# Turning a gated activation by VectorE and small transfers instead of TensorE's transposes

## The chip, the cores and the metric

The kernel runs on one core of one Trainium2 chip. The time is device time in microseconds (us) of one execution, the median of several. Five engines work side by side, each through its own queue of instructions in order: TensorE (PE; its weight loads are shown as PEld), VectorE (DVE), ScalarE (ACT), GpSimd (POOL) and SyncE (SP). SP issues most transfers (DMAs), GpSimd those that accumulate into what they write.

## The reference

Two layers are added to x (8 sequences of 256 tokens, 1024 features). The first is a dense weight plus a mixture of eight low-rank experts, two of them chosen for each token; the second is a dense weight chosen for each sequence.

```python
def _L0_cond_ref(x, language_ids, W, Wr, A, B):       # A: 8 experts x 16 ranks x 1024
    base = jnp.einsum('btd,od->bto', x, W)
    logits = jnp.einsum('btd,ed->bte', x, Wr)
    logits = logits + bias[:, None, :]
    topw, topi = jax.lax.top_k(logits, 2)
    weights = jax.nn.softmax(topw, axis=-1)
    gates = jnp.sum(jax.nn.one_hot(topi, E) * weights[..., None], axis=-2)
    h = jnp.einsum('btd,erd->bter', x, A)
    lora_out = jnp.einsum('bter,bte,eor->bto', h, gates, B)
    return base + SCALING * lora_out

x = x + _L0_cond_ref(x, itok_B_0_7, W, Wr, A, B)
x = x + jnp.einsum('bsi,boi->bso', x, weight[itok_B_0_15])
```

Everything is in 32-bit floats.

## The kernel before

The first layer is one product of 2048 tokens with a 1024 x 1024 weight, done in seven block products after Strassen and Winograd. The tokens fall into two halves of 1024 (j = 0, 1), the features into two halves, so x is four blocks `x11`, `x12`, `x21`, `x22`, and W (with the identity added, which brings in "x +") is four blocks of weights. `opening` does product 1, `product(key, ...)` the others, in the order 2, 5, 6, 3, 7, 4. The sums of x blocks that Winograd's form needs (T1 to T4) are made in place by GpSimd's accumulating transfers: T1 is `x12 += x11` (two copies, line 1018), T2 is `x22 += x12`; `raw` (line 1028) and `add_raw` (line 1022) reload and add x from DRAM for T3 and T4. Output blocks of tokens of half 1 are kept with the sign turned, so what the low-rank part adds there must be turned too.

Inside each product there is a second level of the same scheme: `make_subs` lists VectorE's differences (`s1` to `s4` of weights, `t1` to `t4` of x), and some of its products ("leaves" 2, 3, 4) get a third level, whose differences are `r1` to `r4` and `q1` to `q4` and whose seven matmul pairs are `piece(1)` to `piece(7)`. Matmuls of 128x512 are at line 556, pieces at line 470, VectorE's sums and differences at line 228 (`tt`). `put` and `take` add finished banks of PSUM to the output blocks y (named A6, B5, X2, A7, B3, A4 after the bank and the second-level product).

The low-rank part. `project(j, c)` (line 256) computes for 512 tokens at a time A x and the router's logits together, tokens on the partitions. `take(j, c)` adds the bias to the logits and lets ScalarE copy A x into `hT[j]`: 128 tokens on the partitions, 8 chunks of tokens, 128 columns (8 experts x 16 ranks). `gating(j)` is a list of some 20 small VectorE steps that find the two best experts and their gates, and ends with `onto_h`, one multiply of 128x1024 that puts the gates on `hT[j]`. To use it as the right side of a matmul it must be turned, so that experts and ranks lie on the partitions and tokens in the columns: `turn(j, banks)` does so with 8 TensorE transposes into two banks (line 326) and two ScalarE copies into `hg[j]`, with a factor -1 for half 1. From there on `mm` adds the low-rank part into the same banks as the dense product:

```python
if up is not None and rows is not None:
    steps += [(up[rows][:, ts(m, P)], hg[tokens][:, c, :], m) for m in ms]
```

Half 0 is used in product 2 first, half 1 in product 5 first. `turn(0, ...)` is called after the last projection and before product 2; half 1's gating waits in a queue, and product 2 calls `turn_1` between its leaves.

The order of VectorE's work is planned when the program is built. `now` holds a planner's clock for TensorE and VectorE; `queue` holds work with the events it needs; `ahead` takes from the queue whatever is due before TensorE gets further; `force` takes a piece of work, and all before it that is free, at once. `product` puts its own late differences (`own`) at the head of the queue. [...]

Storage is reused closely: `hT[0]` and `hT[1]` lie in the first half of block `y22`, which product 5 writes; the gating's small tables lie in `y12`.

Of the kernel before, what the change touches and what calls it, by code (L numbers as in the profile page):

```python
# [9 lines left out]
F32 = mybir.dt.float32  # L10
I32 = mybir.dt.int32
AF = mybir.ActivationFunctionType
ALU = mybir.AluOpType
# [3 lines left out]
P = 128  # L17
# [8 lines left out]
def kernel(  # L26
# [62 lines left out]
    def flat(blk):  # L89
        return blk.rearrange("p k n -> p (k n)")  # L90

    def pair(name, n):

        return psum.tile([P, 2, TQ], F32, name=name, tag=f"pair{n}")
# [5 lines left out]
    def halves(pair_):  # L100
        return [pair_[:, v, :] for v in range(2)]
# [21 lines left out]

    aw_sb = flat(yb["12"])[:, : KC * EA].rearrange("p (k e) -> p k e", k=KC)
    hT = [flat(yb["22"])[:, j * C * ER : (j + 1) * C * ER].rearrange("p (c e) -> p c e", c=C) for j in range(2)]

    small = {}

# [92 lines left out]
    def copy(out_, x, scale=1.0):  # L221
        if scale == 1.0:
            nc.scalar.copy(out_, x)
        else:
            nc.scalar.activation(out_, x, AF.Copy, scale=scale)  # L225
# [13 lines left out]
        add(d, d, ident.unsqueeze(1).to_broadcast([P, k1 - k0, P]))  # L239


    hg = [const.tile([ER, 2, TQ], F32, name=f"hg{j}") for j in range(2)]
    lg = [rtile([P, C, E], f"lg{j}") for j in range(2)]
    gate8 = {}

# [43 lines left out]

    def gating(j):  # L290

        m1, hot1, ops1 = first_max(lg[j], j, 1)
        rest = rtile([P, C, E], "rest")
        m2, hot2, ops2 = first_max(rest, j, 2)
        dm = rtile([P, C], "dm")
        ex = rtile([P, C], "ex")
        den = rtile([P, C], "den")
        g1 = rtile([P, C], "g1")
        g2 = rtile([P, C], "g2")
        wide = [P, C, E]  # L300

        def onto_h():
            h = hT[j].rearrange("p c (e r) -> p (c e) r", r=R)
            g = hot1.rearrange("p c e -> p (c e)").unsqueeze(2).to_broadcast([P, C * E, R])
            tt(h, h, g, ALU.mult)


        ops = ops1 + [
            lambda: nc.vector.scalar_tensor_tensor(rest, hot1, NEG, lg[j], ALU.mult, ALU.add)
        ] + ops2 + [  # L310
            lambda: minus(dm, m2, m1),
            lambda: nc.scalar.activation(ex, dm, AF.Exp),
            lambda: nc.vector.tensor_scalar(den, ex, 1.0, None, ALU.add),
            lambda: nc.vector.reciprocal(g1, den),
            lambda: nc.vector.tensor_scalar(g1, g1, SCALING, None, ALU.mult),
            lambda: tt(g2, g1, ex, ALU.mult),
            lambda: tt(hot1, hot1, g1.unsqueeze(2).to_broadcast(wide), ALU.mult),
            lambda: tt(hot2, hot2, g2.unsqueeze(2).to_broadcast(wide), ALU.mult),
            lambda: add(hot1, hot1, hot2),
        ]  # L320
        return [(0.26, f) for f in ops] + [(us(2 * TQ), onto_h)]

    def turn(j, banks):

        for n in range(C):
            nc.tensor.transpose(banks[n // CQ][:, ts(n % CQ, P)], hT[j][:, n, :], ident)  # L326
        for c, ps_g in enumerate(banks):
            copy(hg[j][:, c, :], ps_g, -1.0 if j else 1.0)


    bdiff = const.tile([ER, OG + 3 * OQ], F32, name="bdiff")
# [19 lines left out]
    def us(n):  # L351
        return (n + 66) / 960

    def vec(t, fn, key=None):
        fn()
        now["dve"] += t
        done[key] = now["dve"] + 0.1

    def event(name, later=0.0):
        events[name] = now["pe"] + later  # L360
# [56 lines left out]
    def third(key, leaf, lhs, rhs, place, what):  # L417

        ra = lambda i, j: lhs()[:, j, ts(i, P)]
        rb = lambda i, j: rhs()[:, i, ts(j, NQ)]
        n0, n1 = slice(0, NQ), slice(NQ, TQ)
        t, own = {}, {}
        at = {"r13": 0, "r2": P, "r4": 2 * P, "q13": 3 * P, "q2": 3 * P + NQ, "q4": 3 * P + 2 * NQ}
        me = f"{key}:L{leaf}"

        def op(name, tag, fn, x, y, what):
            width = P if name[0] == "r" else NQ

            def run():
                if place == 0:
                    t[name] = sub3.tile([P, width], F32, name=f"{name}_{key}{leaf}", tag=tag)
                elif place == 3:
                    t[name] = flat(yb["12"])[:, 2048 + at[tag] : 2048 + at[tag] + width]
                else:
                    t[name] = spare(1536 + (place - 1) * 1152 + at[tag], width)
                fn(t[name], *(t[v] if isinstance(v, str) else v() for v in (x, y)))

            return us(width), what, f"{me}.{name}", run  # L440

        A, B = (lambda i, j: lambda: ra(i, j)), (lambda i, j: lambda: rb(i, j))
        ops = [
            op("r1", "r13", add, A(1, 0), A(1, 1), what),
            op("q1", "q13", minus, B(0, 1), B(0, 0), what),
            op("r2", "r2", minus, "r1", A(0, 0), what),
            op("q2", "q2", minus, B(1, 1), "q1", what),
            op("r4", "r4", minus, A(0, 1), "r2", what),
            op("q4", "q4", minus, B(1, 0), "q2", what),
        ]  # L450
        ops3 = [
            op("r3", "r13", minus, A(0, 0), A(1, 0), (f"{me}.5",)),
            op("q3", "q13", minus, B(1, 1), B(0, 1), (f"{me}.5",)),
        ]

        def piece(n, acc=None, banks=None, fresh=False):
            if n in (1, 5):
                own[n] = (single(f"P{n}_{key}{leaf}", n // 5) if banks is None else banks[n // 5])[:, n0]
            for x in {3: ("r4",), 4: ("q4",), 5: ("r1", "q1"), 6: ("r2", "q2", "P1"), 7: ("r3", "q3", "P6")}.get(n, ()):
                force(f"{me}.{x}")  # L460
            out_, l, r = {
                1: lambda: (own[1], ra(0, 0), rb(0, 0)),
                2: lambda: (acc[:, 0, n0], ra(0, 1), rb(1, 0)),
                3: lambda: (acc[:, 0, n1], t["r4"], rb(1, 1)),
                4: lambda: (acc[:, 1, n0], ra(1, 1), t["q4"]),
                5: lambda: (own[5], t["r1"], t["q1"]),
                6: lambda: (own[1], t["r2"], t["q2"]),
                7: lambda: (own[1], t["r3"], t["q3"]),
            }[n]()
            nc.tensor.matmul(out_, lhsT=l, rhs=r, start=(n in (1, 5) or fresh and n in (2, 4)), stop=True, skip_group_check=True)  # L470
            now["pe"] += 0.432
            event(f"{me}.{n}", 0.2)

        def take(n, dest, base=None, sub=False):

            cut = lambda v: {1: v[:, 0, n0], 6: v[:, 0, n1], 5: v[:, :, n1]}[n]
            if n == 7:
                cut = lambda v: v[:, 1, :].rearrange("p (j n) -> p j n", j=2)
            src = own[5 if n == 5 else 1]
            if n in (5, 7):  # L480
                src = src.unsqueeze(1).to_broadcast([P, 2, NQ])
            evict(NQ if n in (1, 6) else TQ, cut(dest), src, None if base is None else cut(base), f"{me}.P{n}", sub)

        return ops, ops3, piece, take
# [61 lines left out]
    def multiply(up=None, tokens=None):  # L546


        def mm(acc, lhs, rhs, first=False, rows=None, c=0, part=(0, 1), ms=(0, 1), need=()):
# [1 line left out]
                force(key)  # L551
            steps = [(lhs[:, k, ts(m, P)], rhs[:, k, :], m) for k in part for m in ms] if part else []
            if up is not None and rows is not None:
                steps += [(up[rows][:, ts(m, P)], hg[tokens][:, c, :], m) for m in ms]
            for i, (l, r, m) in enumerate(steps):
                nc.tensor.matmul(  # L556
                    acc[:, m, :],
# [132 lines left out]
        out(5, q2, q2)  # L690
        add(q2, A, q2)

    def product(key, base, dest, lora=None, tokens=None, sub=False, joined=None, between=None):

# [16 lines left out]
        own = list(deep[2][1]) if 2 in deep else []  # L713
        own += late[:1] + (deep[3][0] if 3 in deep else []) + late[1:] + (deep[4][0] if 4 in deep else [])
        own += (deep[3][1] if 3 in deep else []) + (deep[4][1] if 4 in deep else [])
        queue[:0] = own
        A = new("A")
        mm(A, a(0, 0), b(0, 0), True)
        X = new("X")
        nc.scalar.copy(X, A)  # L720
        if 2 in deep:
            _, _, piece, take = deep[2]
            piece(1)
            take(1, at[0], old[0], sub)
            B = new("B")
            mm(B, t["s1"], t["t1"], True, "1", 1, ms=(0,), need=K("s1", "t1"))
            piece(5)
            mm(A, t["s2"], t["t2"], need=K("s2", "t2"))
            event(f"{key}:P6", 0.2)
# [26 lines left out]
        if 4 in deep:  # L756
            _, _, piece4, take4 = deep[4]
            piece4(1)
            take4(1, at[2], old[2], sub)
        if between is not None:  # L760
            between(X)
        if 3 in deep:
            hold[0] = key
            _, _, piece, take = deep[3]
# [278 lines left out]
    project(1, 1, singles("ps_h_1_1"))  # L1043
    now["pe"] += 7.5
    force("gates0")
    turn(0, halves(pair("ps_g_0", 2)))
    after(0.4, lambda: take(1, 1))
    now["pe"] += 1.8
    for k in (0, 2):
        add_x("12", "11", k, k + 2)  # L1050
    event("T1", 17.0)
# [1 line left out]
        add_x("22", "12", k, k + 2)  # L1053
    event("T2", 30.0)
    queue += [(t, (), f"gate{i}", f) for i, (t, f) in enumerate(gating(1))]
    gates = queue[-1][2]
    queue += make_subs("5", "21", "12", (2, 3, 4), ("T1",), "2", 1)

    def turn_1(X):
        force(gates)  # L1060
        turn(1, halves(X))
        now["pe"] += 1.8

    product("2", y21, y11, 0, 0, between=turn_1)
    raw("21", 0, 1)
    add_raw("21", 1, 1)
    event("T3", 30.0)
# [21 lines left out]
        y0[:] = y0 or prep_y(0)  # L1089
        y0[i][2]()  # L1090

    queue += [(0.6, ("4:P7", "7:join2"), f"4.y{i}", lambda i=i: prep_y0(i)) for i in range(4)]
    product("4", y21, y21, 1, 0)
    for q in list(queue):
        q[3]()
# [58 lines left out]
```

## Time and profile before

| | |
|---|---|
| Median of 3 runs | 424.83 us (424.72 to 425.22) |
| The profiled execution | 424.31 us, of which the span from first to last instruction 422.2 |
| TensorE's granted clock | 1.000 |
| Data moved by transfers | 72.61 MB, mean 172 GB/s |

A span is cut into 40 slices of 10.55 us; each digit is the busy share of a slice in tenths:

```profile
PE   8999999999999999999999999999999999999996
DVE  1977879968789999978799565765657666665531
DMA  8995099576220946928903483765558384640202
```

The transfers' row falls to 0 in the fifth slice (42 to 53 us): the loads of the first layer are done and T1 has not begun. VectorE is at 9 in the slices from 84 us on, in which products 2 and 5 meet. A timeline line reads: start, duration of the group, engine, line, operation, output and inputs by name, size, number of instructions, and in brackets how long the engine was idle before and what ended that. Matmul starts are 0.43 us apart for 128x512, although each is shown 0.59 us long.

### The profile page before, as it was taken

To read this page: it belongs to the slowest core of one execution; us is meant where nothing else is said; L and a number is where in the kernel's file an instruction comes from. 1 tells how busy PE (TensorE), PEld (TensorE's weight loads), DVE (VectorE), ACT (ScalarE), POOL (GpSimd) and SP (SyncE) were. 2 spreads that over 40 slices of the span, in tenths; PEclk is the share of its full clock that TensorE was granted. 3 is DMA by queue.
4 is the path that set the end of the run, shared out by engine and by line. 5 is a ranking of instruction groups with operands and counts; after the bars stand their busy time and mean duration, and the time that the engine had idled before them with its cause. 6 is when DMAs were issued, how large, how long until landed. Compare 5 with 4: busy or idle time off the path is not lost.

```text
span 422.2 us, 3674 instructions
## 1 busy us (share of the span) xinstructions
PE 417.1 (99%) x1318; PEld 230.7 (55%) x1318; DVE 304.8 (72%) x489; ACT 40.9 (10%) x73; POOL 17.6 (4%) x26
## 2 busy tenths in 40 slices
PE   8999999999999999999999999999999999999996
PEld 6679975555655554554555444444444444444574
DVE  1977879968789999978799565765657666665531
ACT  2020130112110000000000101010101101010110
POOL 1000020110001101103000000000000000000000
PEclk9999999999999999999999999999999999999999
DMA  8995099576220946928903483765558384640202
GB/s 273 384 397 245 0 186 199 127 186 101 99 99 8 166 140 165 262 57 165 332 0 102 150 313 134 263 224 211 199 201 296 113 307 178 229 170 2 99 0 99
DMA packets 20257, 72.61 MB, mean 172 GB/s; under 512 B 1552, under 2 KB 3856, under 8 KB 15248
## 3 DMA queue, kind: packets, MB, share of 16 engines
q1 hardware_dynamic: 15088, 58.87, 38.4%
q0 software_dynamic: 3904, 12.58, 16.5%
q10 hardware_dynamic: 1248, 0.93, 0.7%
q8 instruction: 10, 0.16, 0.2%
q14 instruction: 7, 0.06, 0.1%
HBM read 55.61 MB, written 8.39 MB: 152 GB/s over the span
## 4 chain that ended last, share of the span: by engine, by line
PE 99%; POOL 0%; ACT 0%; issue 0%; POOLq 0%
PE A L908 23%; PE A L556 20%; PE B L908 13%; PE B L556 11%; PE ps_h L256 7%; PE X L908 7%; PE P L470 6%; PE A_last L975 3%; PE X L470 3%; PE X L556 3%; PE A L470 2%; PE B L470 1%; PE idle L573 1%; PE X L326 0%; PE ps_g L326 0%; ACT z L1005 0%
## 5 line engine op out<-in xcount | busy, mean ns | idle before, releaser
L556 PE MATMUL A<-t,s 128*128 128x512 f32 x112 | 50.3, 592 | 0.0
L908 PE MATMUL B<-x,x 128*128 128x512 f32 x96 | 43.2, 592 | 0.0
L228 DVE TENSOR_TENSOR w<-w,w 128x1024 f32<-128x1024 f32 x24 | 29.0, 1223 | 15.1 <-PE A L908 15.1
L908 PE MATMUL A<-w,x 128*128 128x512 f32 x88 | 39.6, 592 | 0.0
L908 PE MATMUL A<-w,y 128*128 128x512 f32 x88 | 39.1, 592 | 0.0
L256 PEld LDWEIGHTS ps_h<-y,x 128*128 128x128 f32 x256 | 31.7, 190 | 2.9 <-issue 2.4
L556 PEld LDWEIGHTS A<-t,s 128*128 128x128 f32 x112 | 21.2, 190 | 20.8 <-issue 20.1
L256 PE MATMUL ps_h<-y,x 128*128 128x136 f32 x256 | 31.9, 279 | 0.0
L908 PEld LDWEIGHTS B<-x,x 128*128 128x128 f32 x96 | 18.2, 190 | 22.1 <-issue 21.8
L228 DVE TENSOR_TENSOR y<-A,y 128x1024 f32<-128x1024 f32 x18 | 22.0, 1222 | 9.3 <-PE A L556 5.8
L908 PEld LDWEIGHTS A<-w,x 128*128 128x128 f32 x88 | 16.7, 190 | 21.0 <-issue 21.0
L908 PEld LDWEIGHTS A<-w,y 128*128 128x128 f32 x88 | 16.7, 190 | 20.6 <-issue 20.6
L228 DVE TENSOR_TENSOR y<-P,y 128x512 f32<-128x512 f32 (+1 forms) x37 | 21.1, 572 | 8.0 <-PE P L470 6.2
L556 PE MATMUL A<-x,w 128*128 128x512 f32 x56 | 25.3, 592 | 0.0
L228 DVE TENSOR_TENSOR x<-w,x 128x1024 f32<-128x1024 f32 (+1 forms) x12 | 10.9, 911 | 10.8 <-PE A L908 7.8
L228 DVE TENSOR_TENSOR w<-x,w 128x1024 f32<-128x1024 f32 x8 | 9.7, 1225 | 10.2 <-PE A L908 5.6
L225 ACT ACTIVATE z<-A 128x512 f32<-128x512 f32 x12 | 7.2, 597 | 101.0 <-PE A L908 101.0
L228 DVE TENSOR_TENSOR z<-z,X 128x512 f32<-128x512 f32 x7 | 4.8, 687 | 15.9 <-PE X L908 15.9
L556 PEld LDWEIGHTS A<-x,w 128*128 128x128 f32 x56 | 10.4, 190 | 10.3 <-issue 10.0
L556 PE MATMUL B<-x,s 128*128 128x512 f32 x32 | 14.9, 592 | 0.0
L228 DVE TENSOR_TENSOR x<-x 128x1024 f32<-128x1024 f32 (+1 forms) x15 | 14.7, 1005 | 0.0
L720 ACT COPY X<-A 128x1024 f32<-128x1024 f32 x6 | 6.0, 997 | 89.8 <-PE A L556 89.8
(203 smaller groups left out, 591.6 us busy)
## 6 DMA issues: line engine op xcount, KB each, us to landing
x<-w_dram SPq DMA_DIRECT2D x24, 1024.0 KB, 5.5
x<-xT_dram SPq DMA_DIRECT2D x10, 1024.0 KB, 11.0
w<-w_dram SPq DMA_DIRECT2D x8, 1024.0 KB, 4.7
out_dram<-z SPq DMA_DIRECT2D x15, 512.0 KB, 3.0
x<-x POOLq DMA_DIRECT2D x4, 1024.0 KB, 9.9
x<-xT_dram POOLq DMA_DIRECT2D x4, 1024.0 KB, 9.1
y<-y POOLq DMA_DIRECT2D x8, 512.0 KB, 5.1
w<-wT_dram SPq DMA_DIRECT2D x3, 1024.0 KB, 15.1
```

What stands on the lines that cost most here:

```text
L225: nc.scalar.activation(out_, x, AF.Copy, scale=scale)
L228: nc.vector.tensor_tensor(out_, x, y, op)
L256: nc.tensor.matmul(ps[v][:, u * EA : (u + 1) * EA], lhsT=xk(k, j, c)[:, ts(r, P)], rhs=aw_sb[:, k, :], start=(first and k == some[0] and u ...
L470: nc.tensor.matmul(out_, lhsT=l, rhs=r, start=(n in (1, 5) or fresh and n in (2, 4)), stop=True, skip_group_check=True)
L556: nc.tensor.matmul(acc[:, m, :], lhsT=l, rhs=r, start=(first and i < len(ms)), stop=(i >= len(steps) - len(ms)), skip_group_check=True,)
L573: nc.tensor.matmul(idle[:, 0, :P], lhsT=ident, rhs=ident, start=True, stop=True)
L720: nc.scalar.copy(X, A)
L908: nc.tensor.matmul(accs[name], lhsT=lhs[:, k // 2, k % 2, :], rhs=rhs[:, k, :], start=(first and k == 0), stop=(k == KH - 1), skip_group_c ...
L975: nc.tensor.matmul(acc, lhsT=lhs[:, k // 2, k % 2, :], rhs=rhs[:, k, ts(v, m)], start=(first and k == 0), stop=(k == KH - 1), skip_group_c ...
```

## The change

The turn of `hT[j]` no longer uses TensorE. VectorE turns each square of 32 x 32 by itself (one instruction for all of a half) into `squares[j]`, in the second half of block `y22`; 16 transfers of 32 partitions x 256 values, issued by SP, move the squares to the partitions where they belong. The layout of `hg[j]` becomes 4 groups of partitions-to-be x 8 chunks x 32 tokens, and `turned(j, c)` reads 512 tokens of it in runs of 32. The factor -1 of half 1 goes into the gates.

Further parts of the same change:

- `turn(j)` is now the last entry of `gating(j)`, so it is done by VectorE's order: for half 0 ahead of the differences of product 2, for half 1 out of the queue.
- Ahead of T1's transfers GpSimd copies one column of `hg[0]`, and so waits for all 16 landings of half 0.
- `product` puts its own late work behind those entries of the queue that begin with its key, and ahead of the others. In product 2 the first half of B's matmuls, with its low-rank part, stands ahead of `piece(1)`; in the others behind it as before.
- VectorE's work gives events too (`vec`), and `r3` and `q3` of a leaf wait for `r2` and `q2` as well.
- The sums of y for the first adapter wait for the last piece of leaf 3 in product 4 instead of its seventh second-level product.

```diff
+    QS = P // 4
+    squares = [flat(yb["22"])[:, (2 + j) * C * ER : (3 + j) * C * ER] for j in range(2)]
...
-    hg = [const.tile([ER, 2, TQ], F32, name=f"hg{j}") for j in range(2)]
+    hg = [const.tile([ER, 4, C, QS], F32, name=f"hg{j}") for j in range(2)]
...
-            lambda: nc.vector.tensor_scalar(g1, g1, SCALING, None, ALU.mult),
+            lambda: nc.vector.tensor_scalar(g1, g1, -SCALING if j else SCALING, None, ALU.mult),
...
-        return [(0.26, f) for f in ops] + [(us(2 * TQ), onto_h)]
-
-    def turn(j, banks):
-
-        for n in range(C):
-            nc.tensor.transpose(banks[n // CQ][:, ts(n % CQ, P)], hT[j][:, n, :], ident)
-        for c, ps_g in enumerate(banks):
-            copy(hg[j][:, c, :], ps_g, -1.0 if j else 1.0)
+        return [(0.26, f) for f in ops] + [(us(2 * TQ), onto_h), (us(2 * TQ), lambda: turn(j))]
+
+    def turn(j):
+
+
+        nc.vector.transpose(squares[j], hT[j].rearrange("p n (b r) -> p b n r", b=4))
+        v = squares[j].rearrange("p (b n) -> p b n", b=4)
+        for a in range(4):
+            for b in range(4):
+                nc.sync.dma_start(
+                    hg[j][b * QS : (b + 1) * QS, a].rearrange("p n q -> p (n q)"), v[a * QS : (a + 1) * QS, b]
+                )
+
+    def turned(j, c):
+        return hg[j][:, :, c * CQ : (c + 1) * CQ, :].rearrange("p a n q -> p n a q")
...
-        done[key] = now["dve"] + 0.1
+        done[key] = events[key] = now["dve"] + 0.1
...
-            op("r3", "r13", minus, A(0, 0), A(1, 0), (f"{me}.5",)),
-            op("q3", "q13", minus, B(1, 1), B(0, 1), (f"{me}.5",)),
+            op("r3", "r13", minus, A(0, 0), A(1, 0), (f"{me}.5", f"{me}.r2")),
+            op("q3", "q13", minus, B(1, 1), B(0, 1), (f"{me}.5", f"{me}.q2")),
...
-                steps += [(up[rows][:, ts(m, P)], hg[tokens][:, c, :], m) for m in ms]
+                steps += [(up[rows][:, ts(m, P)], turned(tokens, c), m) for m in ms]
...
-        queue[:0] = own
+        rest = list(queue)
+        queue[:] = [q for q in rest if q[2].startswith(key)] + own + [q for q in rest if not q[2].startswith(key)]
...
             _, _, piece, take = deep[2]
+            B = new("B")
+            if key == "2":
+                mm(B, t["s1"], t["t1"], True, "1", 1, ms=(0,), need=K("s1", "t1"))
             piece(1)
             take(1, at[0], old[0], sub)
-            B = new("B")
-            mm(B, t["s1"], t["t1"], True, "1", 1, ms=(0,), need=K("s1", "t1"))
+            if key != "2":
+                mm(B, t["s1"], t["t1"], True, "1", 1, ms=(0,), need=K("s1", "t1"))
...
-        if between is not None:
-            between(X)
...
     force("gates0")
-    turn(0, halves(pair("ps_g_0", 2)))
     after(0.4, lambda: take(1, 1))
-    now["pe"] += 1.8
+
+    landed = const.tile([ER, 4], F32, name="landed")
+    nc.gpsimd.tensor_copy(landed, hg[0][:, :, 0, 0])
     for k in (0, 2):
         add_x("12", "11", k, k + 2)
...
-    product("2", y21, y11, 0, 0, between=turn_1)
+    product("2", y21, y11, 0, 0)
...
-    queue += [(0.6, ("4:P7", "7:join2"), f"4.y{i}", lambda i=i: prep_y0(i)) for i in range(4)]
+    queue += [(0.6, ("4:L3.7", "7:join2"), f"4.y{i}", lambda i=i: prep_y0(i)) for i in range(4)]
```

More of the change, by code (lines that the diff above doesn't have):

```diff
@@ L691, in opening, with product @@
         add(q2, A, q2)
-    def product(key, base, dest, lora=None, tokens=None, sub=False, joined=None, between=None):
+    def product(key, base, dest, lora=None, tokens=None, sub=False, joined=None):
         a, b, t, late, deep = subs.pop(key)
@@ L1055 @@
     queue += [(t, (), f"gate{i}", f) for i, (t, f) in enumerate(gating(1))]
-    gates = queue[-1][2]
     queue += make_subs("5", "21", "12", (2, 3, 4), ("T1",), "2", 1)
[L1059 to L1062, printed above, removed]
-    product("2", y21, y11, 0, 0, between=turn_1)
+    product("2", y21, y11, 0, 0)
     raw("21", 0, 1)
```

## The prediction

> **What bounds the kernel now.** I read the busy table and the chain of waits first, to learn which engine sets the end, then the timeline from 50 to 97 us, where the two turns stand, then the list of transfers and SP's first issues for what a small transfer costs.
>
> From the page, the busy table and the chain:
>
> ```profile
> PE 417.1 (99%) x1318; PEld 230.7 (55%) x1318; DVE 304.8 (72%) x489; ACT 40.9 (10%) x73; POOL 17.6 (4%) x26
> ...
> PE 99%; POOL 0%; ACT 0%; issue 0%; POOLq 0%
> ```
>
> TensorE is busy for 417.1 of 422.2 us and is the whole chain. So a matmul taken away is worth its time, if nothing new makes TensorE wait; and a new wait of TensorE costs its length. The question is only whether the turned values arrive in time.
>
> The timeline around the two turns (start, us, engine, line, operation; matmul starts are what to read, since their ends overlap):
>
> ```profile
> 51.73 1.22 DVE L228 TENSOR_TENSOR y<-y,y 128x1024 f32<-128x1024 f32 x1
> 52.86 0.91 POOL L1018 DMA_DIRECT2D x<-x  x1 [50.06 <-PE ps_h L256]
> 52.88 0.68 DVE L228 TENSOR_TENSOR s<-w 128x512 f32<-128x512 f32 x1
> 57.95 1.04 PE L326 MATMUL ps_g<-ident,y 128*128 128x128 f32 x8
> 58.83 2.74 PE L556 MATMUL A<-x,w 128*128 128x512 f32 x6
> 60.77 0.85 POOL L1018 DMA_DIRECT2D x<-x  x1 [5.21 <-DMA x<-x]
> 62.26 0.59 PE L470 MATMUL P<-x,w 128*128 128x256 f32 x2
> 62.69 1.88 PE L556 MATMUL B<-t,s 128*128 128x512 f32 x4
> 64.41 1.02 PE L556 MATMUL B<-hg,b_sb 128*128 128x512 f32 x2
> 66.88 0.85 POOL L1018 DMA_DIRECT2D x<-x  x1 [5.25 <-DMA x<-x]
> 78.97 1.22 DVE L228 TENSOR_TENSOR x<-x 128x1024 f32<-128x1024 f32 x1
> 79.45 1.04 PE L326 MATMUL X<-ident,y 128*128 128x128 f32 x8
> 80.32 1.88 PE L556 MATMUL B<-x,s 128*128 128x512 f32 x4
> 91.43 1.22 DVE L228 TENSOR_TENSOR y<-A,y 128x1024 f32<-128x1024 f32 x1
> 93.64 1.88 PE L556 MATMUL B<-x 128*128 128x512 f32 x4
> 95.36 1.02 PE L556 MATMUL B<-hg,b_sb 128*128 128x512 f32 x2
> ```
>
> The reader is to see: the last gating step of half 0 starts at 51.73, six microseconds before TensorE turns the half; the turned half is first used at 64.41; the accumulating copies of T1 start at 52.86.
>
> SP's first three issues (start, us for all three), and a small store in the list of transfers (us from issue to landing):
>
> ```profile
> 0.75 1.34 SPq L144 DMA_DIRECT2D x<-xT_dram  x3
> ```
>
> ```profile
> out_dram<-z SPq DMA_DIRECT2D x1, 128.0 KB, 1.9
> ```
>
> One issue takes 0.39 to 0.43 us alone, so three in 1.34 give a step of some 0.47 us; the later stores' issues take 0.35, so a step of about 0.40 is the low side.
>
> [...] no transpose of VectorE is in this trace, a 128x1024 operation takes 1.22 us. [...] no matmul here reads its moving operand in short pieces, so no run shows it.
>
> **The change part by part.** Everything on TensorE before 57.95 is untouched.
>
> *Removed from TensorE.* 8 transposes from 57.95 to 58.83 (0.88 us) and 8 from 79.45 to 80.32 (0.87): 1.75 us, all on the path. ScalarE loses 4 copies (1.07 + 1.09 us); it is 10% busy, worth nothing in itself.
>
> *Half 0, supply.* VectorE's order before the turn is the same, so its multiply ends where the next operation now starts, 52.88. The transpose, taken at 1.22 us, ends at 54.10. SP has no transfer between its load of the weights at 21.95 and one at 73.19, so it waits with nothing ahead. 16 issues at 0.47 us: the last starts 15 x 0.47 = 7.05 us later, at 61.15, and lands 1.9 us after, at 63.05. With a step of 0.40 it is 62.0. The ninth reuses the first one's semaphore, 3.8 us after it, which has landed by then. The data, 32 KB a transfer, come to 70 GB/s at this step, below the 210 GB/s that the copies of T1 reached here; and T1 itself is held back, so the transfers meet no other.
>
> *Half 0, demand.* Product 2 starts 0.88 us earlier, and its first piece (0.43 us, 62.26 to 62.69) now stands behind B's first half. So B's use of hg moves from 64.41 to 64.41 - 0.88 - 0.43 = 63.10, its weights 0.43 before. Supply and demand coincide. TensorE must also see eight semaphores of transfers. I take a stall of 0.25 us; bounds 0 (step 0.40) and 4 us (transpose 2.4, step 0.6, landing 3).
>
> *VectorE behind the turn.* It ran without a gap from 46 to 60.6 us, so the read-out of ps_h_1_1 at 60.40 moves by about 1.2 to 61.6, ScalarE's copies to 62.5. The first piece, which overwrites that bank, would start at 63.97: covered by 1.4 us. At its old place, 61.4, it would have waited about 1 us, so the moved piece belongs to the gain.
>
> *T1.* GpSimd's small copy waits for all 16 landings, so T1's two copies start at about 63.3 instead of 52.86 and 54.71. Then the first lands about 7.9 us later at 71, the second near 76 (the first T2 copy shows the first landing at 60.7, the second T2 copy the other at 66.8), T2 near 85. Behind them on GpSimd's queue stand only the raw additions of x21, at 80.83 before. The first reader of T1 on VectorE stood at 78.97 for the differences of product 5; after the change these come later, near 84, behind the second turn. T1 has 8 us in hand and costs nothing; without this cover each us would stop VectorE for one.
>
> *Half 1.* The gating is now spread further: its last steps and its multiply come behind A7 and the first piece of leaf 4. With the trace's steps (1.15 for 128x1024, 0.60 for 512, 0.33 for 256, 0.25 for a small one) I walk VectorE from the take of the first piece at 64.6: eight small ones and two differences to 68.3, A6 to 69.6, B5 to 72.8, leaf 4 to 74.4, the take of leaf 2 to 76.4, X2 to 77.5, A7 to 79.5, the multiply to 81.7, the transpose to 82.9. SP's 16 issues land by 82.9 + 7.05 + 1.9 = 91.9, a little later if T2 is still moving. Product 5 needs this half at 95.36 - 1.75 = 93.6: hidden by 1.7 us. The same walk ends A4, which frees a bank for product 5's B, at 91.0; B starts at 93.64 - 1.75 = 91.9. Hidden by 0.5 to 0.9 us; a transpose of 2.4 us would take that away and cost up to 1.
>
> *SP behind the second turn.* The loads of x21 at 73.19 now wait behind 32 transfers, so to about 90. GpSimd's additions to it go from 80.83 and 92.89 to about 97 and 99, landed near 110. x21 is next read for product 7, whose differences start after 130: nothing.
>
> *The strided read.* 64 matmuls read hg, now in runs of 32 values (128 bytes) instead of 512. Taken at nothing[...]; if it cost 27 ns in each of the 64, the gain would be gone.
>
> *The end of product 4.* The four sums for the first adapter move behind the last piece. VectorE then waits about 1.2 us for TensorE there and the weights' differences, ready at 231.1 for a use at 232.88, keep some 0.6 us: nothing.
>
> **Sum.** -1.75 + 0.25 = -1.5 us. Against the profiled execution's own 424.31 us that is 422.8; that execution lies 0.5 below the median of the runs, 424.83, so the forecast in terms of the runs is 423.3.
>
> **The rivals.**
> *Half 0 arrives late enough to give the gain back.* For it: supply and demand meet within 0.1 us, and 16 serial issues are the longest term. A step of 0.55 us makes 15 x 0.08 = 1.2 us more stall, a slower landing 0.5: -1.75 + 0.25 + 1.7 = +0.2, 425.0. Against it: 0.47 is measured in this trace at its busiest time.
> *Slower, the wait on hg[0] takes the place of the transposes.* If the transpose streams at half rate, or each issue with its own semaphore takes 0.6 us, hg[0] lands at 54.1 + 1.2 + 9 + 2 = 66.3; TensorE stands 3.2 us at B's first half: 424.83 - 1.75 + 3.2 = 426.3. From a landing at 65.7 on the kernel is slower by over 0.2%. For it: neither the transpose nor 16 small issues in a row is in the trace. [...]
> *The strided operand is slow.* At double the time (0.43 us more in 64 matmuls) +27 us, 452; at a tenth of it +1. [...]
> *Everything is hidden:* a step of 0.40, -1.75, 423.1; counted with the forecast.
>
> **How the numbers follow.** About 0.2% (0.85 us) is what a measurement of this kernel can tell from no change: faster means below 423.98, that is, a stall under 0.9. Forecast with everything hidden 0.54, its own range 422.7 to 424.0; half 0 giving the gain back 0.22; slower by the wait 0.18; slower by the strided read or VectorE's longer queue 0.06. The range for 8 in 10 runs from 422.7 to 426.2.
>
> **What would show it.** Right: no transposes on TensorE, product 2 at 57.95, B's hg matmul at 63.1 to 63.6 with a gap of a few tenths, SP's 16 issues at a step of 0.4 to 0.5 from 54.2, T1 at 63 to 64, hg matmuls at 592 ns as before, and TensorE ahead by a constant 1.5 us from 64 on to the end. Wrong: a gap of microseconds ahead of B's hg matmul at 63, a VectorE transpose well over 1.3 us, gaps at product 5's B, or longer hg matmuls.

## The result: slower, and the profile after

| | before | after |
|---|---|---|
| Median of 6 runs | 424.77 us (423.61 to 425.22) | 428.52 us (427.26 to 429.33) |
| Ratio to before, with its interval | | 1.0089 (1.0066 to 1.0112) |
| The profiled execution | 424.31 us | 427.40 us |
| Its span | 422.2 us | 425.6 us |
| Mean granted clock of TensorE | 1.000 | 0.996 |

The changed kernel is 0.9% slower; 423.3 us was forecast, and 428.52 lies above the forecast's range, which ended at 426.2.

The page of after, busy table, TensorE's row in the 40 slices and its granted clock, and the chain of waits:

```profile
PE 416.8 (98%) x1302; PEld 229.4 (54%) x1302; DVE 307.1 (72%) x491; ACT 38.6 (9%) x69; POOL 17.8 (4%) x27
...
PE   8999988999999999999999999999999999999996
...
PEclk9999998999999999999999999999999999999999
...
PE 89%; DVE 4%; SPq 4%; issue 1%; DMA 1%; ACT 0%; POOL 0%; POOLq 0%; DVEq 0%
```

Three things changed. TensorE executes 16 matmuls less, but its busy time falls by only 0.3 us. The row of PE has an 8 in the sixth and seventh slices (53 to 74 us), and the clock an 8 in the seventh. And TensorE is no longer the whole chain: it now runs through VectorE, SP's queue and the transfers into hg, once for the turn of half 0 and once for that of half 1.

The timeline of after around that turn:

```profile
52.30 1.25 DVE L330 STREAM_TRANSPOSE y<-y 128x1024 f32<-128x1024 f32 x1
53.57 10.79 SPq L334 DMA_DIRECT2D hg<-y  x16
57.24 3.60 PE L567 MATMUL A<-x,w 128*128 128x512 f32 x8
60.68 1.88 PE L567 MATMUL B<-t,s 128*128 128x512 f32 x4
60.95 0.25 DVE L230 TENSOR_TENSOR y<-ps_h,bias 128x16 f32<-128x16 f32 x2
65.84 2.05 PE L567 MATMUL B<-hg,b_sb 128*128 128x512 f32 x2 [3.28 <-DMA hg<-y]
66.36 1.79 POOL L1031 DMA_DIRECT2D x<-x  x2 [0.33 <-issue]
67.67 1.06 PE L481 MATMUL P<-x,w 128*128 128x256 f32 x2
...
68.77 0.42 DVE L230 TENSOR_TENSOR y<-P,y 128x256 f32<-128x256 f32 x1 [7.57 <-PE P L481]
69.27 3.60 PE L567 MATMUL A<-t,s 128*128 128x512 f32 x8
```

VectorE's transpose is as fast as forecast. SP then needs 10.79 us for 16 issues. B's four matmuls are started every 0.43 us from 60.68, so TensorE could have gone on at 62.40; it goes on at 65.84, which is a stall of 3.44 us. And what follows is slow: from 65.84 to 69.27 stand two matmuls of 512 and four of 256, 1.72 us at the usual pace, and they take 3.43. TensorE's clock over three stretches of after (start:end, us; TensorE's busy time and matmuls; granted clock; busy share of the transfer engines and GB/s) shows the pace:

```profile
57.00:62.00 5.00, 5.00 (x16) 1.00 0.20 45
65.84:69.27 3.43, 3.43 (x7) 0.52 0.58 115
69.27:73.00 3.73, 3.73 (x11) 1.00 0.95 191
```

After the stall the granted clock is at half (0.52) for about 3.4 us. That costs 3.43 - 1.72 = 1.71 us more. The clock is at 0.50 already in the 0.1 us before TensorE goes on at 65.84, and T1's first copy is issued only at 66.36, so T1's traffic doesn't bring the half pace. It doesn't come in every execution either: one of the six of after has a mean clock of 1.000 (427.26 us, the shortest; there is no trace of it), the others 0.995 or 0.996.

SP's issues in after, three of the 16 one by one:

```profile
55.49 0.59 SPq L334 DMA_DIRECT2D hg<-y  x1
...
56.13 1.26 SPq L334 DMA_DIRECT2D hg<-y  x1
...
63.77 0.59 SPq L334 DMA_DIRECT2D hg<-y  x1
```

An issue takes 0.59 us, the next starts 0.64 after it (55.49 to 56.13; 0.635 on average), and one of the 16 took 1.26. The last starts at 63.77 and its data are used at 65.84.

The second turn, the timeline of after and the waits of PE (engine, line, releaser: us in total, times, longest):

```profile
86.16 1.25 DVE L330 STREAM_TRANSPOSE y<-y 128x1024 f32<-128x1024 f32 x1
87.44 10.02 SPq L334 DMA_DIRECT2D hg<-y  x16
96.34 1.88 PE L567 MATMUL B<-x 128*128 128x512 f32 x4
97.55 1.08 SPq L1041 DMA_DIRECT2D x<-xT_dram  x2
98.93 1.10 PE L567 MATMUL B<-hg,b_sb 128*128 128x512 f32 x2 [0.71 <-DMA hg<-y]
```

```profile
PE B L567 <- DMA hg<-y: 4.0, 2, 3.3
```

Product 5 waits for hg[1] too: its matmul would have started at 96.34 + 4 x 0.43 = 98.06 and starts at 98.93, 0.87 us late. These two are TensorE's only waits for hg.

**The balance.** Transposes gone -1.75, stall of product 2 +3.44, half pace behind it +1.71, stall of product 5 +0.87: together +4.27 us. Product 2 began at 57.24, 0.71 before the 57.95 at which the transposes began in the execution of before, in a part that the change doesn't touch, so +3.56 is expected in the span; it grew by 3.4.

### The profile page after: what moved, and what is told of

The parts are those of the page before. It is cut to its first block, busy times and chain, and to the rows that moved or that the text cites. A ratio compares the mean times of both kernels' runs of the same rounds, so it can differ in the third digit from the quotient of the medians.

```text
span 425.6 us, 3693 instructions
## 1 busy us (share of the span) xinstructions
PE 416.8 (98%) x1302; PEld 229.4 (54%) x1302; DVE 307.1 (72%) x491; ACT 38.6 (9%) x69; POOL 17.8 (4%) x27
## 4 chain that ended last, share of the span: by engine, by line
PE 89%; DVE 4%; SPq 4%; issue 1%; DMA 1%; ACT 0%; POOL 0%; POOLq 0%; DVEq 0%
PE A L921 23%; PE A L567 17%; PE B L921 13%; PE B L567 10%; PE X L921 6%; PE P L481 5%; SPq L334 4%; PE A_last L988 3%; PE ps_h L259 3%; PE X L481 3%; PE X L567 2%; DVE y L230 2%; PE A L481 1%; PE B L481 1%; DMA hg<-y 1%
## 5 line engine op out<-in xcount | busy, mean ns | idle before, releaser
L567 PE MATMUL A<-t,s 128*128 128x512 f32 x112 | 50.3, 592 | 0.0
L230 DVE TENSOR_TENSOR w<-x,w 128x1024 f32<-128x1024 f32 x8 | 9.7, 1225 | 10.2 <-PE A L921 5.6
L481 PE MATMUL P<-q,r 128*128 128x256 f32 x48 | 14.6, 386 | 0.0
```

The lines of the kernel that those rows point to most:

```text
L230: nc.vector.tensor_tensor(out_, x, y, op)
L567: nc.tensor.matmul(acc[:, m, :], lhsT=l, rhs=r, start=(first and i < len(ms)), stop=(i >= len(steps) - len(ms)), skip_group_check=True,)
```

## The experiments

Ratios are against before, each with its interval. "From A to A" is the time from product 2's first matmul of A to product 5's: 30.95 us before (58.83 to 89.78), 35.23 after (57.24 to 92.47). The kernels differ from after by the edit alone, unless the text says otherwise.

**late_lora: the same turn, used later.** The pass over hg in B goes behind the last dense pass, so that the data have some 6 us more.

```diff
-                mm(B, t["s1"], t["t1"], True, "1", 1, ms=(0,), need=K("s1", "t1"))
+                mm(B, t["s1"], t["t1"], True, ms=(0,), need=K("s1", "t1"))
...
-            mm(B, t["s1"], t["t1"], True, "1", 1, ms=(1,))
+            mm(B, t["s1"], t["t1"], True, ms=(1,))
+            mm(B, None, None, False, "1", 1, part=())
```

> Edit: in each product with leaf 2, the low-rank matmuls of bank B are put behind both halves of B's dense matmuls, so hg[0] is first needed some 6 us later (about 69 instead of 62.4) and hg[1] likewise. Theory (the waits for the landed squares, 3.4 us in product 2 and 0.9 us in product 5, and the half-speed stretch of TensorE behind the first one, 1.7 us, are the whole loss): all three go and the removed transposes remain as a gain, before - 1.75 = 423.0 us, within 0.6. Rival 1 (the changed order of VectorE's work or the strided reads of hg cost something of their own): above 424.8. Rival 2 (the half-speed stretch is not caused by the gap): 424.7 with a stretch of long matmuls left near 66 us.

Measured: 422.07 us, ratio 0.9948 (0.9936 to 0.9960). It beats both kernels. Its timeline:

```profile
66.48 0.19 POOL L1063 COPY landed<-hg 128x4 f32<-128x4 f32 x1 [63.67 <-DMA hg<-y]
...
69.38 1.88 PE L567 MATMUL B<-hg,b_sb 128*128 128x512 f32 x4
71.09 0.59 PE L481 MATMUL X<-x,w 128*128 128x256 f32 x2
```

GpSimd's copy, which waits for all 16 landings, starts at 66.48; TensorE first uses hg at 69.38 and goes on without a gap (4 x 0.43 = 1.72, up to 71.09). From A to A takes 30.08 us, 0.87 less than before: the removed transposes of half 1; those of half 0 stood ahead of A. So the gain of 1.75 was there, and the whole loss lies in the lateness of hg.

**issue_cost: what one issue costs.** To the kernel before, 20 transfers are added on SP in its idle time; nothing reads what they write. Four go from SBUF to SBUF over 128 partitions, eight from SBUF to SBUF over 32 as in the change, eight from DRAM to 32 partitions.

```diff
+    for i in range(4):
+        nc.sync.dma_start(room[:, i * 256 : (i + 1) * 256], bdiff[:, i * 256 : (i + 1) * 256])
+    for i in range(8):
...
+        nc.sync.dma_start(
+            room[q * 32 : (q + 1) * 32, 1024 + h * 256 : 1280 + h * 256], bdiff[f * 32 : (f + 1) * 32, h * 256 : (h + 1) * 256]
+        )
+    for i in range(8):
...
+        nc.sync.dma_start(
+            room[q * 32 : (q + 1) * 32, 1536 + h * 256 : 1792 + h * 256], xT[0, 0, 0, 0][q * 32 : (q + 1) * 32, h * 256 : (h + 1) * 256]
+        )
```

> The kernel before with 20 extra transfers on SP in its idle time after the opening, which nothing reads: 4 of 128 partitions x 256 values within SBUF, 8 of 32 partitions x 256 values within SBUF (as the change has them), 8 of 32 partitions x 256 values from DRAM. Measures SP's step from issue to issue. Theory A (32 partitions make the issue long): both groups of 32 step by 0.63 us, the group of 128 by 0.45. Theory B (source and destination both in SBUF make it long): both SBUF groups 0.63, the group from DRAM 0.45. Theory C (waiting for landings sets it): steps grow only behind the eighth transfer.

Measured in one execution, by line of the kernel (shortest, median and longest issue in ns, first and last start in us):

```profile
L1034 SPq DMA_DIRECT2D y<-bdiff x4: 540/561/586, 43.3 to 45.3; - x4
```

```profile
L1038 SPq DMA_DIRECT2D y<-bdiff x8: 581/589/592, 45.9 to 50.3; - x8
```

```profile
L1043 SPq DMA_DIRECT2D y<-xT_dram x8: 419/420/1195, 51.0 to 54.4; - x8
```

With both ends in SBUF an issue took 0.59 us over 32 partitions and 0.56 over 128; with its source in DRAM 0.42. As steps from start to start, the first kind gives (50.3 - 45.9) / 7 = 0.63 us, which is the step of the change. So here neither the number of partitions nor the semaphores make the difference: where the data lie does (0.59 against 0.42). One issue of the third kind took 1.2 us, like the odd one of half 0 in after; what makes such a one was not tried.

**keep_warm and keep_warm4: the half pace.** Matmuls of no use, into a bank that nobody reads, are put where TensorE stands idle in after, for 3.28 us by the bracket: 7 in the first kernel, 4 in the second. The traces show each of 128x512 in f32 as two passes of 0.43 us (the 4 stand as x8 in the timeline below), so 7 fill 6.0 us and not the 3.0 that I had meant.

```diff
-                mm(B, t["s1"], t["t1"], True, "1", 1, ms=(0,), need=K("s1", "t1"))
+                mm(B, t["s1"], t["t1"], True, ms=(0,), need=K("s1", "t1"))
+                warm = single("warm", 0)
+                for i in range(4):
+                    nc.tensor.matmul(warm, lhsT=ident, rhs=b(0, 0)[:, 0, :], start=True, stop=True)
+                mm(B, None, None, False, "1", 1, part=(), ms=(0,))
```

> Edit: seven matmuls of 128x512 into an unused bank fill the gap ahead of the first low-rank matmuls of product 2 (7 x 0.43 = 3.0 of the 3.4 us); the wait itself stays. Theory (TensorE's clock falls to half because it stood idle for over 3 us): the stretch from 65.8 to 69.3 runs at full rate, 1.7 us less than the change, about 426.8 us. Rival (the matmuls there are slow because T1's transfers start at the same moment, or because the new layout of hg is slow to read at first): no gain, 428.5 us or a little more.

Measured with 7: 429.07 us, ratio 1.0103 (1.0089 to 1.0117). The clock stayed at 1.000, but the fill ran from 63.20 to 69.21 past the landing at 67.04, so 2.2 us were lost to it and the time, 0.5 us above after's, is what a loss of 2.2 and a gain of 1.7 make, but also the rival's "a little more": it decides nothing. With 4:

> As keep_warm, with four matmuls (8 passes of 0.43 = 3.4 us) in the gap instead of seven, which ran past the landing by 2.2 us. Theory (the idle gap of over 3 us makes the clock fall): the low-rank matmuls follow at full rate, 1.7 us less than the change, about 426.8 us. Rival (something else slows TensorE at 66 us): 428.5 us as the change.

Measured: 426.94 us, ratio 1.0063 (1.0045 to 1.0081). Its timeline, and TensorE's clock just behind the fill (columns as above):

```profile
62.85 3.60 PE L740 MATMUL warm<-x,ident 128*128 128x512 f32 x8
66.28 1.02 PE L567 MATMUL B<-hg,b_sb 128*128 128x512 f32 x2
67.14 0.59 PE L481 MATMUL P<-x,w 128*128 128x256 f32 x2
```

```profile
66.28:68.00 1.72, 1.72 (x7) 1.00 0.00 0
```

B's pass over hg starts 8.58 us behind A, as in after (8.60), so the data come no sooner; but the work that took 3.43 us there takes 1.72 here. From A to A is 33.51, that is 1.72 less than after. About 0.6 us of it is given back in product 5, where the wait for hg[1] grows to 1.3. T1's copies are issued as close behind the landing as in after. The mean clock is 1.000 in all six executions of keep_warm4. So it is TensorE's idleness (3.28 us in after, at 0.52 behind it), and nothing in the matmuls on hg or in T1's traffic, that brings the half pace here.

**no_hold: T1's transfers not made to wait.** GpSimd's small copy that waits for hg is left out.

```diff
-    landed = const.tile([ER, 4], F32, name="landed")
-    nc.gpsimd.tensor_copy(landed, hg[0][:, :, 0, 0])
```

> Edit: GpSimd's small copy ahead of T1's transfers is taken out, so T1 starts at about 52 as in the kernel before. Theory (SP's serial issue sets the landing of hg[0], not the traffic): landing later by under 1 us, 428.5 to 429.5. Rival (the traffic of T1 delays each small transfer, and the ninth to sixteenth wait for the first eight): landing later by 3 us and more, 431 to 436. If the hold itself costs: under 428.

Measured: 441.26 us, ratio 1.0397 (1.0383 to 1.0411): far from the "under 1 us" of my theory, and above the rival's 431 to 436 too. Its timeline, and two of its issues:

```profile
53.27 0.91 POOL L1031 DMA_DIRECT2D x<-x  x1 [50.47 <-PE ps_h L259]
...
54.67 23.07 SPq L334 DMA_DIRECT2D hg<-y  x16
...
79.79 2.05 PE L567 MATMUL B<-hg,b_sb 128*128 128x512 f32 x2 [16.11 <-DMA hg<-y]
```

```profile
55.34 1.35 SPq L334 DMA_DIRECT2D hg<-y  x1
...
77.10 0.64 SPq L334 DMA_DIRECT2D hg<-y  x1
```

Beside the accumulating copies the issue itself grows: 16 of them take 23.07 us, and from the second to the last the step is (77.10 - 55.34) / 14 = 1.55 us, against 0.635 in after; only the first and the last are short. From the start of the last issue to the use of its data pass 79.79 - 77.10 = 2.69 us, against 65.84 - 63.77 = 2.07 in after. So holding T1 back is worth some 13 us here; the transfers' own time is the smaller part of it.

**two_queues: two engines issue.** Six of half 0's transfers go to GpSimd and eight of half 1's to ScalarE.

```diff
-                nc.sync.dma_start(
+                n = 4 * a + b
+                other = n % 8 in (2, 5, 7) if j == 0 else n % 2
+                queue_ = (nc.scalar if j else nc.gpsimd) if other else nc.sync
+                queue_.dma_start(
```

> Edit: of the 16 transfers of half 0, six go through GpSimd's queue and ten through SP's; of half 1, eight each through ScalarE's and SP's; nothing else is changed. Theory (SP's step of 0.63 us within SBUF, times 16, sets the landing): half 0 lands at about 53.5 + 10 x 0.63 + 1.9 = 61.8, ahead of its use at 62.4; half 1 lands 5 us earlier; both waits go and the time is that of late_lora or 0.5 more, 422 to 423.5. Rival (the transfers themselves, all on the same 16 DMA engines, set it): as the change, 428.5.

Measured: 422.31 us, ratio 0.9949 (0.9934 to 0.9963). Its timeline:

```profile
54.66 7.04 SPq L337 DMA_DIRECT2D hg<-y  x10
54.93 2.99 POOL L337 DMA_DIRECT2D hg<-y  x6 [52.11 <-DVE y L330]
...
61.77 1.88 PE L570 MATMUL B<-t,s 128*128 128x512 f32 x4
63.61 1.10 PE L570 MATMUL B<-hg,b_sb 128*128 128x512 f32 x2
```

SP's ten are out by 61.7, GpSimd's six, at 0.5 us each, by 57.9. B's pass over hg starts at 63.61, 0.1 us behind 61.77 + 1.72: no stall, no half pace, and no wait for hg in product 5. There was nothing to spare: against the use the landing came 0.65 us later than I had reckoned, since one of SP's ten took 1.32 us. The order of work is that of after. So serial issue is enough to explain the loss.

**half1_only and half0_only: one turn at a time.** Each gives the other half back to TensorE, with its transposes at their old places. In half1_only T1 isn't held and the first piece stands ahead of B, as before.

```diff
-        return [(0.26, f) for f in ops] + [(us(2 * TQ), onto_h), (us(2 * TQ), lambda: turn(j))]
+        return [(0.26, f) for f in ops] + [(us(2 * TQ), onto_h)] + ([(us(2 * TQ), lambda: turn(j))] if j else [])
...
     force("gates0")
+    turn_pe(0, halves(pair("ps_g_0", 2)))
```

> Edit: half 0 is turned by TensorE as before (T1 not held back, piece(1) ahead of B), half 1 by VectorE and the 16 transfers. Theory: 8 transposes less (-0.87) and a wait of 0.9 to 1.5 us for hg[1] in product 5: 424.2 to 425.2. Rival (half 1 holds a good part of the loss, by VectorE's changed order or the delayed loads of x21): over 426.

Measured: 423.13 us, ratio 0.9967 (0.9954 to 0.9979), and no wait for hg[1], where I expected 0.9 to 1.5 us. Its timeline:

```profile
75.58 1.25 DVE L339 STREAM_TRANSPOSE y<-y 128x1024 f32<-128x1024 f32 x1
76.86 10.11 SPq L343 DMA_DIRECT2D hg<-y  x16
...
93.08 1.88 PE L578 MATMUL B<-x 128*128 128x512 f32 x4
```

The 16 issues are as slow as ever, but they begin 16 us ahead of product 5's B and not 9. With the first piece back at its old place, VectorE's order puts the whole gating of half 1 ahead of A6, and the transpose comes 16.4 us behind product 2's A (59.13), where late_lora has it 23.8 behind (81.55 and 57.78). So this kernel changed more than I had meant, and says nothing of why after waits in product 5.

> Edit: half 1 is turned by TensorE as before (between the leaves of product 2), half 0 by VectorE and the 16 transfers. Theory: -0.87, the wait of 3.4 us and the half-speed stretch of 1.7 us: 428.0 to 429.2, nearly all of the change's loss. Rival: under 427.

Measured: 432.88 us, ratio 1.0193 (1.0169 to 1.0216), worse than both turns together. Its timeline:

```profile
66.51 2.05 PE L578 MATMUL B<-hg,b_sb 128*128 128x512 f32 x2 [3.62 <-DMA hg<-y]
69.45 0.42 DVE L230 TENSOR_TENSOR y<-P,y 128x256 f32<-128x256 f32 x1 [7.93 <-PE P L492]
...
86.85 1.97 PE L329 MATMUL X<-ident,y 128*128 128x128 f32 x8 [3.01 <-DVE y L230]
88.61 2.71 PE L578 MATMUL B<-x,s 128*128 128x512 f32 x4
```

VectorE stands still for 7.9 us while TensorE stalls, since its next work is the result of the first piece. Half 1's gating then comes too late for TensorE's transposes, which wait 3.0 us, and these and the matmuls behind them run at half pace a second time (8 transposes take 88.61 - 86.85 = 1.76 us, 0.87 before; the granted clock is 0.51 from 86.80 to 89.00). The first stall isn't what makes the gating late, since it holds back both engines alike. In two_queues, which has no such stall, TensorE would be free for the transposes at 78.72 + 0.43 = 79.15 (behind the first piece of leaf 4), but VectorE goes on from the gating to its own transpose only at 82.30, 3.15 us later. It is the change's order of VectorE's work, with the end of the gating behind A7 and that piece, which doesn't suit a turn by TensorE. So this kernel doesn't price half 0 alone.

**split_half0 and split_half1: why hg[1] was late.** After half1_only two causes were open: the stall of product 2, or the same slow issue. Each kernel shares out one half's transfers as two_queues does, and leaves the other on SP.

The edits are to two_queues; first split_half0:

```diff
-                queue_ = (nc.scalar if j else nc.gpsimd) if other else nc.sync
+                queue_ = nc.gpsimd if other and not j else nc.sync
```

> Only half 0's transfers are shared out (10 on SP, 6 on GpSimd), so the stall of product 2 goes; half 1's 16 stay on SP. Theory A, hg[1] was late because 16 issues within SBUF at 0.63 us take 2.4 us more than my step allowed and its margin was 1.7: the wait in product 5 stays although product 2 has no stall: half 1's transpose at 82 to 83, 16 issues in 10 us or more (13.4 in the kernel with the late low-rank pass), landing near 95 against a need near 94.2, a wait of 0.6 to 4 us; about 423.0 to 426.5. Theory B, the stall of product 2 made half 1 late: no wait on hg[1], 422.3 like the kernel with both halves shared out.

Measured: 423.39 us, ratio 0.9970 (0.9957 to 0.9983). TensorE's only wait for hg is in product 5:

```profile
PE B L570 <- DMA hg<-y: 0.8, 1, 0.8
```

Then split_half1:

```diff
-                queue_ = (nc.scalar if j else nc.gpsimd) if other else nc.sync
+                queue_ = nc.scalar if other and j else nc.sync
```

> Only half 1's transfers are shared out (8 on SP, 8 on ScalarE); half 0's 16 stay on SP, so the stall of 3.4 us and the half pace of product 2 stay. Theory A: half 1's issues take 6 us instead of 10, no wait on hg[1] in product 5, so 0.9 us less than the changed kernel: about 427.6. Theory B: the wait of 0.7 to 0.9 us in product 5 stays, since the stall of product 2 is there: 428.5.

Measured: 426.75 us, ratio 1.0044 (1.0027 to 1.0061). Its timeline:

```profile
65.48 1.30 PE L570 MATMUL B<-hg,b_sb 128*128 128x512 f32 x2 [2.59 <-DMA hg<-y]
...
96.04 1.88 PE L570 MATMUL B<-x 128*128 128x512 f32 x4
97.76 1.02 PE L570 MATMUL B<-hg,b_sb 128*128 128x512 f32 x2
```

The wait in product 5 is there without the stall of product 2 and is gone with it (96.04 + 1.72 = 97.76). So half 1 was late for the same reason as half 0, the slow issue. My figure for this kernel, 427.6, was 0.9 too high: the stall here is 2.6 and not 3.3 (both by the brackets), since none of half 0's 16 issues is an odd one: the last starts 9.5 us behind the first, and not 10.2.

## Why the prediction was wrong, by its own steps

- *Removed from TensorE, -1.75 us: right.* late_lora and two_queues, in which hg is in time, gain about that and a little more (ratios 0.9948 and 0.9949, some 2.2 us, with intervals down to 1.7 and 1.6).
- *VectorE's transpose at 1.22 us: right*, 1.25. The 1.22 was an estimate, from the other operations of 128x1024 in before.
- *"16 issues at 0.47 us": this is the step that failed.* The price was read off SP's first three issues, which load from DRAM, and was used for transfers within SBUF. These take a step of 0.635: fourteen such steps and one of 1.31 (the odd issue) put the last issue 10.20 us behind the first, where the sum had 7.05. Of the 3.15 us between, 15 x 0.165 = 2.5 is the kind of transfer and 0.67 the odd issue, which is luck of the execution: split_half1 has none. "Against it: 0.47 is measured in this trace at its busiest time" was an argument about how busy the queue is; it missed that the measured issues were of another kind. The semaphores were no part of it: in the trace of after the 16 transfers of a half use eight of them, each twice, and the ninth issue, the first that reuses one, takes 0.59 us like its neighbours.
- *Landing 1.9 us: right.* The list of transfers of after, in its last column:

```profile
hg<-y SPq DMA_DIRECT2D x32, 32.0 KB, 1.9
```

- *Demand at 63.10: right.* B's first pass ended at 62.40 in an execution that ran 0.71 ahead. With the supply 3.15 us later, "Supply and demand coincide" became a stall of 3.44 where 0.25 was taken.
- *"A new wait of TensorE costs its length": wrong for the long one.* It cost 3.44 + 1.71. The sum had no term for the granted clock, nor had the rival with a stall of 3.2 us. In after the bracket gives an idle gap of 3.28 us ahead of the half pace; in split_half1 2.59 us was already enough (TensorE's clock was 0.61 from 65.48 to 68.91), and 1.28 us in product 5 of keep_warm4 was not (mean clock 1.000). The length of the gap isn't all: in split_half1 the clock was still at 1.00 for the first 0.76 us after TensorE had gone on, and fell only at 66.24. So no bound in microseconds is shown.
- *Half 1 "hidden by 1.7 us": wrong by the same term.* The walk of VectorE was right: it put the end of the transpose at 82.9, and late_lora has it starting at 81.55 and SP's issues at 82.82. (In the row of before VectorE is at 9 from 63 to 84 us, in product 2, and at 6 in the slice behind, not at 9 from 84 us on.) But 15 x 0.16 = 2.4 us more of issuing exceeds 1.7, and 0.7 is late; 0.87 was measured, 0.8 in split_half0.
- *T1 costs nothing: right.* It started at 66.36 and not 63.3, and only T2, on GpSimd, waited for it. But a later T1 isn't free for the second turn: in late_lora, where T2's second copy was issued at 79.64, half 1's 16 issues took 13.36 us from 82.82 on, against 10.02 in after (I take it that the copy was still moving, since copies of this kind land after a median of 9.6 us in after); the later use hid that.
- *"The transfers meet no other": right only because T1 is held*; no_hold shows 16 us of waiting without it. I had put no price on that.
- *SP behind the second turn, nothing: right.* x21's loads were issued at 97.55 and not at 90; no wait for them followed.
- *The strided read, nothing: right.* That was an estimate; matmuls on hg take 592 ns as before.
- *The bank that A4 frees, and the end of product 4, nothing: right.* Product 5's B starts at 96.34 without a wait, and the balance above leaves nothing for the end of product 4.
- *The read-out of ps_h_1_1 at 61.6: right*, 60.95, which is 61.66 after adding 0.71, although VectorE did have three gaps of 0.3 to 0.4 us between 46 and 60.6 us in before.

The rival "the wait on hg[0] takes the place of the transposes" was what happened, and its step of 0.6 for the issue was near. That its stall of 3.2 is so near 3.44 is luck: it named a slow transpose or slow issues, but its landing of 66.3 adds both, 1.2 for a transpose that was not slow. With the step alone it lands at 65.1, a stall of 2.0, and comes to 425.1; with the half pace and half 1 (1.71 + 0.87), which it lacked, to 427.7, against 428.52.

## What to carry to other kernels

Price an issue by transfers of the same kind: where no row of the trace has both ends in SBUF, the nearest row is only a guess, and 16 in a row multiply what it misses. Let two engines issue, or put the pass over a late operand last in its accumulation; each turned this loss of 0.9% into a gain of 0.5%. And a stall of TensorE can cost more than its length: those of 2.59 and 3.28 us (the brackets of split_half1 and after) cost, in most executions here, another 1.7 us of half pace (granted clock 0.52 in after).

## What the runs showed that I had not expected

An issue on SP took 0.59 us with both ends in SBUF over 32 partitions, 0.56 over 128, and 0.42 with the source in DRAM (issue_cost). Beside accumulating copies the step from issue to issue rose from 0.635 us to 1.55 (no_hold). Now and then a single issue took 1.2 or 1.3 us without them (1.26 in after, 1.32 in two_queues); why is open. After gaps of 2.59 us (split_half1) and 3.28 us (after) TensorE lost about 1.7 us at half its pace, and after the 16.11 us of no_hold it ran at half pace (0.50 from 79.79 to 83.30) for some 5.2 us in all, that is 2.6 us lost. The stall in after also left VectorE without work for 7.6 us, where split_half0, without the stall, has 2.7.
